# A four-layer convolution block on one core: the transfers of layer 2's mixing stage, put in the program's order and given other places in the loop

## The chip, the cores and the metric

The kernel runs on one core of one Trainium2 chip. The metric is the device time of one execution in microseconds (us). A core has five engines that follow their own instruction streams and meet through semaphores: PE (matrix multiply; its weight loads are listed apart as PEld), DVE and ACT (elementwise work), POOL (elementwise work) and SP, which here only issues transfers (DMAs) between the core's memory and the chip's large memory. "Granted clock" is the share of PE's full clock that the chip allowed. A name with a line, such as L970, is a line of the kernel before.

## The reference, cut to what matters

Sixteen images of 16 channels and 256x256 points go through four layers, each `x = x + layer(groupnorm(x))`. Layers 0, 1 and 3 are convolutions. Layer 2 is a Laplace operator in the frequency domain, and its part that matters here is this:

```python
alpha = jnp.fft.fft2(x, axes=(-2, -1))
A = 1.0 / (omega1[:, None, None, None] - weights_pole1[None])
Bm = 1.0 / (omega2[:, None, None, None] - weights_pole2[None])
S = jnp.einsum('ikpq,oikp,xikq->oxik', weights_residue, A, Bm)
output_residue1 = jnp.einsum('biox,oxik->bkox', alpha, S)
```

For every pair of frequencies (o, x), a 16x16 complex matrix S mixes the 16 input channels of `alpha` into 16 output channels, for all images. This is the "mixing". Because the input is real, only 129 of the 256 frequencies x are computed.

## The kernel before, in words

The kernel is one program of five stages, one after the other: layers 0 and 1; layer 2's forward transform, which writes `alpha` to a scratch tensor `alphad`; layer 2's mixing, which reads `alphad` and writes `mixd`; layer 2's transform back, which reads `mixd`; and layer 3. The change is in the third, the mixing (L860 to L1022).

**Rows.** The mixing runs over 64 steps, `for n in range(NF)` at L963, here called rows; one row is four frequencies o with all their 129 frequencies x. A row multiplies a tile `z` (128 partitions, `alpha` of the row) by a tile `sk` (the matrices S of the row). There are two `z` tiles, `zs[0]` and `zs[1]`; row n uses `zs[n % 2]`. Two matrices S are made at a time, for rows 2m and 2m+1, while the two rows before them are mixed.

**Groups.** A row has 32 positions (`for at in range(PX)`), four small products each (L970, written to `ps_m`), and so four groups g = 0 to 3 of eight positions. At the end of a group ACT copies half of `ps_m` to `other` (L996), and DVE adds and subtracts the two halves into the row's result tile `ob` (two instructions, L998, listed under the helper's line L190). `ps_m` has two buffers, `ob` has two.

**Making S beside it.** Each `next(steps, None)` runs one step of the generator `system` (L876): eight matmuls of one tile `ps_s` on PE (L891), then two steps that copy it into `sk`, on ACT (L899, L903, L908) for three tiles of four and on DVE for the fourth (`turns = "ADAA"`). One group takes three such steps, so one tile.

**Transfers of a row.** `reload(n, f)` (L927) brings in one quarter of the `z` tile of row n: DVE sets one column of that quarter (`V.memset`, L930), and SP issues the load of 258 KB (L917). `leave(n, part)` (L920) has SP issue the store of one quarter of `ob` of row n, 256 KB (L924). A row has four loads and four stores. In row n the program calls `reload(n + 1, 0)`, `leave(n - 1, 1)`, `reload(n + 1, 1)` and `leave(n - 1, 2)` at the end of group 0, `reload(n + 1, 2)`, `leave(n - 1, 3)` and `reload(n + 1, 3)` at the end of group 1, and `leave(n, 0)` at the end of group 3.

**What sets the order.** Instructions of an engine named in `tc.manual_schedule` stand in the order in which the program calls them; for the others a scheduler decides. Before, PE, DVE, ACT and POOL are named and SP is not. In the program as built, SP's stream in this stage is, for every row, four loads L917 and then four stores L924. Each engine works through its stream in order, and a transfer waits on SP for what it needs; a transfer also waits there for the one that stands eight transfers ahead of it, whose semaphore it uses again. A load of `z` needs PE to be done with the tile; a product needs all four loads of its row; a write to `ob` needs the four stores of the row two before.

**First and last rows.** Row 0's tile holds two rows of padding values which POOL clears at the end of row 0 (L992). Rows 62 and 63 have no S to make. After row 63 the stage leaves its last stores and the next stage's tables are loaded.

## Time and profile before

| | |
|---|---|
| time, median of 3 runs (lowest to highest) | 4326.98 us (4321.13 to 4331.19) |
| the profiled execution: its own time, its span | 4332.44 us, 4330.7 us |
| granted clock over the span | 0.955 |
| the mixing stage's rows 2 to 62 | 2302 to 3007 us of the span |
| transfers issued in these 705 us | 244 loads of `z`, 246 stores of `ob`, 186 GB/s |

The profile is of one execution. Its page gives each engine's busy time, and groups of instructions with the idle time of the engine just before them and what ended it. The view of the waits sums these idle times by who waited for whom. A wait "<-issue" is idle time for which the profile shows no cause. The timeline lists instructions in order of time, merged where they are alike; the number in brackets is the idle time before. Matmuls are pipelined on PE, so the durations of single matmuls overlap and a row "x64 in 1.10 us" is a run of 64.

### The profile page before, as it was taken

The page shows a single profiled execution, that of the slowest core. Times are in us where ns is not written, and L with a number is a line of the kernel's source. Part 1 is how long each engine was busy: PE and PEld are TensorE (multiplying, and loading weights), DVE is VectorE, ACT ScalarE, POOL GpSimd, SP SyncE. Part 2 cuts the span into 40 slices and gives each one's busy share as a digit, 9 for nine tenths or more (in the row PEclk, how much of TensorE's full clock was granted, in tenths as well). Part 3 has the DMA queues.
Part 4 walks back from the last instruction along what each step waited for, and adds up shares of the span by engine and source line. Part 5 has one row for each costly group of instructions (what it writes and reads, how often), then busy time and mean ns, then how long its engine had stood idle before and what let it go on. Part 6 is the DMA issues. An engine that isn't in the chain of part 4 may idle for free. (4 is left out here: it accounts for less than half of the span.)

```text
span 4330.7 us, 126404 instructions
## 1 busy us (share of the span) xinstructions
PE 3739.1 (86%) x52880; PEld 2882.1 (67%) x52880; DVE 3040.5 (70%) x5585; ACT 2573.2 (59%) x3641; POOL 2057.0 (47%) x3279
## 2 busy tenths in 40 slices
PE   4999999999967989999996777776899999996776
PEld 1455555555545989899985555555788888883444
DVE  4676667666659878787765566664567777768888
ACT  2868686776824434344446666665545544447898
POOL 2233232423244645564546666664566666662222
PEclk9999999999988999999999999998999999997989
DMA  6767676776633544444535666666878888877998
GB/s 141 172 154 191 142 192 150 183 169 155 158 89 117 164 144 144 139 152 157 162 113 167 182 194 183 185 192 174 228 217 239 237 244 235 247 206 273 343 351 295
DMA packets 479579, 820.78 MB, mean 190 GB/s; under 512 B 39648, under 2 KB 371424, under 8 KB 463584
## 3 DMA queue, kind: packets, MB, share of 16 engines
q1 hardware_dynamic: 431904, 644.63, 52.6%
q0 software_dynamic: 47104, 168.06, 13.0%
q8 instruction: 416, 6.82, 0.7%
q14 instruction: 155, 1.27, 0.1%
HBM read 408.85 MB, written 336.07 MB: 172 GB/s over the span
## 5 line engine op out<-in xcount | busy, mean ns | idle before, releaser
L382 PE MATMUL ps<-va,wt 128*64 128x512 f32 (+1 forms) x1632 | 668.7, 571 | 11.6 <-POOL va L354 9.2
L382 PE MATMUL ps<-vb,wt 128*64 128x512 f32 (+1 forms) x1632 | 667.1, 570 | 4.5 <-DMA vb<-va 4.5
L781 ACT ACTIVATE y<-ps_y,bc 128x384 f32<-128x384 f32 x512 | 296.4, 581 | 406.8 <-PE ps_y L779 406.6
L403 ACT ACTIVATE v<-xt,nm 32x2048 f32<-32x2048 f32 x248 | 497.2, 2005 | 9.8 <-PE ps L417 3.5
L417 PE MATMUL ps<-v,w1s 128*64 128x259 f32 x4096 | 486.4, 397 | 11.0 <-DVE v L401 6.7
L970 PE MATMUL ps_m<-z,sk 128*32 128x64 f32 x16384 | 334.5, 227 | 176.1 <-issue 126.5
L190 POOL TENSOR_TENSOR w<-rq 128x512 f32<-128x512 f32 x256 | 335.7, 1333 | 261.5 <-ACT rq L1115 259.4
L970 PEld LDWEIGHTS ps_m<-z,sk 128*32 128x32 f32 x16384 | 302.9, 114 | 227.2 <-issue 151.9
L382 PEld LDWEIGHTS ps<-va,wt 128*64 128x64 f32 x1632 | 223.1, 137 | 311.3 <-issue 283.3
L417 PEld LDWEIGHTS ps<-v,w1s 128*64 128x64 f32 x4096 | 338.9, 142 | 136.0 <-issue 27.9
L1114 PE MATMUL ps_o<-exp,fs 128*128 128x128 f32 x2048 | 399.6, 277 | 9.7 <-ACT fs L1162 9.7
L1113 PE MATMUL ps_o<-c_last,zt 128*128 128x128 f32 x2048 | 398.1, 276 | 0.0
L190 DVE TENSOR_TENSOR ob<-ps_m,other 128x256 f32<-128x256 f32 x512 | 192.9, 418 | 276.0 <-ACT other L996 262.4
L1259 PE MATMUL ps_c<-q,wt 64*64 64x512 bf16 (+1 forms) x4608 | 292.8, 405 | 108.6 <-ACT o L1306 91.7
L1113 PEld LDWEIGHTS ps_o<-c_last,zt 128*128 128x128 f32 x2048 | 323.2, 193 | 60.8 <-issue 60.8
L891 PE MATMUL ps_s<-t,l 128*32 128x258 f32 x4096 | 320.5, 401 | 42.3 <-issue 24.8
L190 POOL TENSOR_TENSOR acc<-acc,prod 128x256 f32<-128x256 f32 x240 | 232.8, 970 | 226.4 <-DVE prod L190 220.3
L1259 PEld LDWEIGHTS <-wt 64*64 64x64 bf16 x4800 | 181.6, 114 | 220.2 <-issue 152.8
L1114 PEld LDWEIGHTS ps_o<-exp,fs 128*128 128x128 f32 x2048 | 313.7, 194 | 11.3 <-ACT fs L1162 11.3
L776 PE MATMUL ps_y<-c_y,qd 128*128 128x128 f32 x2048 | 316.0, 277 | 1.6 <-ACT hat L738 1.6
L779 PE MATMUL ps_y<-hat,qd 128*128 128x128 f32 x2048 | 314.5, 276 | 0.0
L190 DVE TENSOR_TENSOR xt<-xt,ps 128x512 f32<-128x512 f32 x256 | 175.4, 685 | 187.6 <-PE ps L382 185.6
(234 smaller groups left out, 8897.9 us busy)
## 6 DMA issues: line engine op xcount, KB each, us to landing
xt<-x2d SPq DMA_DIRECT2D x256, 512.0 KB, 4.3
z<-alphad SPq DMA_DIRECT2D x258, 258.0 KB, 4.0
xt<-in_x_dram SPq DMA_DIRECT2D x256, 256.0 KB, 7.4
x2d<-x2s POOLq DMA_DIRECT2D x256, 256.0 KB, 5.0
mixd<-ob SPq DMA_DIRECT2D x256, 256.0 KB, 4.5
ot<-mixd SPq DMA_DIRECT2D x256, 256.0 KB, 6.2
x3d<-xt SPq DMA_DIRECT2D x128, 512.0 KB, 5.4
xt<-x3d SPq DMA_DIRECT2D x64, 1024.0 KB, 9.4
```

Source lines behind the costliest of these rows:

```text
L190: eng.tensor_tensor(o, a, b, op)
L382: nc.tensor.matmul(ps[halves[h], lo:hi, :], lhsT=wt0[:, w, :], rhs=v[:, 2 * t + lo : 2 * t + hi, j : j + N], start=j == 0 and k == 0, stop ...
L403: nc.scalar.activation(to, o.xt[c][q_], AF.Identity, bias=o.g.nm[q_, 1:2])
L417: nc.tensor.matmul(ps[halves[h], k, 0:U], lhsT=o.w1[:, w : w + 64], rhs=v1[:, lo : lo + U], start=first_, stop=not first_)
L776: nc.tensor.matmul(to[:, :, a, :], lhsT=v[:, c, a, i % 2, :], start=a == 0, stop=a == 1, rhs=y1[:, a].rearrange("p (r f) -> p r f", r=2))
L779: nc.tensor.matmul(ps[:, 2 * P : 3 * P], lhsT=v[:, c, a, i % 2, :], start=False, stop=a == 1, rhs=hats[0][:, a, i].rearrange("p r k -> p ( ...
L781: nc.scalar.activation(y[:, c, :], ps[:, 0 : 3 * P], AF.Copy, scale=bc2[:, b, i // 2, 0:1])
L891: nc.tensor.matmul(ps[at : at + 32, d, 0 : 2 * NX], lhsT=ls[h][:, k + d - k0, n], rhs=t2[:, h, k + d].rearrange("p r x -> p (r x)"), start ...
L970: nc.tensor.matmul(to, lhsT=sk[:, x_], rhs=z[:, :, x_], start=True, stop=True)
L1113: nc.tensor.matmul(ps[:, a, c, :], lhsT=zts[d][:, a, c, :], rhs=last[:, c, :], start=True, stop=False)
L1114: nc.tensor.matmul(ps[:, a, c, :], lhsT=fs[:, d, a, :], rhs=ey[:, d, c, :], start=False, stop=True)
L1259: nc.tensor.matmul(o, lhsT=wt[half[h], w, :], rhs=src, start=i == 0, stop=i == len(work[0]) - 1)
```

## The change

SP is put among the engines that keep the program's order in the mixing stage, and the calls are moved. The loads of row n+2, which go into the tile that row n has just used, now begin at the end of group 3 of row n. The order that SP gets, from the end of row n on, is load 0, store 0, load 1 at group 3 of row n; load 2, store 1, load 3 at group 0 of row n+1; and stores 2 and 3 of row n, which stand in the program at group 1 of row n+1 and need nothing that is not there before.

```diff
         es.enter_context(tc.manual_schedule(engines={
-            mybir.EngineType.PE, mybir.EngineType.DVE, mybir.EngineType.Activation, mybir.EngineType.Pool}))
+            mybir.EngineType.PE, mybir.EngineType.DVE, mybir.EngineType.Activation, mybir.EngineType.Pool,
+            mybir.EngineType.SP}))
...
-                    if n and g < 2:
-                        reload(n + 1, 2 * g)
-                        leave(n - 1, 2 * g + 1)
+                    if n and g == 0:
+                        reload(n + 1, 2)
+                        leave(n - 1, 1)
+                    if g == 3:
+                        reload(n + 2, 0)
+                        leave(n, 0)
...
                     next(steps, None)
-                    if n and g < 2:
-                        reload(n + 1, 2 * g + 1)
                     if n and g == 0:
+                        reload(n + 1, 3)
+                    if n and g == 1:
                         leave(n - 1, 2)
+                        leave(n - 1, 3)
                     if g == 3:
-                        leave(n, 0)
+                        reload(n + 2, 1)
```

In the programs as built, the streams of PE, ACT and POOL hold the same instructions in the same order before and after. DVE's differs in where the four one-column `memset` of a row stand, SP's in the order of its loads and stores. After the last row, SP's stream before has three of the next stage's small table loads ahead of row 63's four stores; after, these three stand behind them.

## The prediction

> **What bounds the kernel now.** I read the page first, then the busy time of the mixing rows, then who waits there, then the timeline of single rows.

> ```profile
> span 4330.7 us, 126404 instructions
> ...
> PE 3739.1 (86%) x52880; PEld 2882.1 (67%) x52880; DVE 3040.5 (70%) x5585; ACT 2573.2 (59%) x3641; POOL 2057.0 (47%) x3279
> ```

> The change touches one stage, so the page's averages decide nothing. The busy times of rows 2 to 62 alone (columns: stretch, its length, then busy us and count of PE, PEld, DVE, ACT and POOL, granted clock, DMA share, GB/s):

> ```profile
> 2302.00:3007.00 705.00, 505.41 (x19590) 409.43 (x19594) 419.07 (x1212) 478.34 (x1145) 423.48 (x1016) 0.96 0.64 186
> ```

> PE is busy 72% of the stage, ACT 68%, the transfers 64%. No engine is full. 64 rows end, by ACT's `other` copies, 11.5 us apart. What fills the rest is in the waits of the same stretch (us in total, times, longest), first PE's, then ACT's, then PEld's:

> ```profile
> PE ps_m L970 <- issue: 125.7, 88, 3.9
> PE ps_m L970 <- ACT sk L908: 31.2, 30, 1.7
> PE ps_s L891 <- issue: 24.8, 19, 2.1
> PE ps_m L970 <- DMA z<-alphad: 15.0, 16, 2.2
> ```

> ```profile
> ACT other L996 <- issue: 111.3, 65, 3.2
> ```

> ```profile
> PEld ps_m L970 <- ACT sk L908: 47.8, 34, 2.2
> ```

> The change can reach one of these directly, the 15.0 us in which PE waits for a load of `z`. The rest of PE's idle time is (a) "issue", 125.7 + 24.8 = 150.5 us, and (b) the wait of the even rows for ACT's last copy into `sk`. ACT in turn waits once in a row (65 times, 1.7 us each) for a product that PE has not issued, so a stop of PE does reach the other engines.

> What "issue" is, the packet records of the trace show. The queue of instructions carries these packets in the stage:

> ```profile
> q8 instruction: 155, 2.54, 1.5%
> ```

> That is 16 KB each. On the page there are 416 with 6.82 MB, and PE has 105,760 instructions: 64 bytes each, 256 in a packet. I read them as refills of PE's instructions. 154 of them start between 2302 and 3004; PE stops for 161 us in all, and starts again some 2.2 to 2.6 us after the packet's start: 1.05 us a refill. The stop goes with the traffic: 0.39 us where fewer than 5 data packets overlap the refill's first 0.9 us (27 refills), 0.82 with 5 to 30 (42), 1.08 with 30 to 60 (34), 1.49 with 60 to 90 (37), 1.73 with more (14). So moved transfers can also move this larger term.

> **The wait that goes.** SP's own timeline around rows 28 to 30:

> ```profile
> 2614.75 2.75 SPq L924 DMA_DIRECT2D mixd<-ob  x4
> 2617.61 4.22 SPq L917 DMA_DIRECT2D z<-alphad  x4
> 2626.26 1.64 SPq L924 DMA_DIRECT2D mixd<-ob  x2
> ```

> The four stores go as soon as a row ends; the four loads come behind, and each waits for its `memset`, the last until group 1 is done. Over rows 2 to 63 the last load is issued 3.0 to 6.9 us (mean 4.2) ahead of its row's first product, and a load of this kind lands 4.1 us after issue (2.8 to 5.8). In 27 of 62 rows the first product starts within 0.65 us of the last load's last packet; 25 of these are odd rows. Even rows wait for ACT's `sk` instead. Row 51 (odd), on PE:

> ```profile
> 2864.11 1.09 PE L970 MATMUL ps_m<-z,sk 128*32 128x64 f32 x60 [1.30 <-issue]
> 2865.04 1.66 PE L891 MATMUL ps_s<-t,l 128*32 128x258 f32 x16
> 2868.41 1.10 PE L970 MATMUL ps_m<-z,sk 128*32 128x64 f32 x64 [1.71 <-DMA z<-alphad]
> ```

> The eight matmuls for S are done, the products wait 1.71 us for the load. A refill began at 2865.25, so part of these 1.71 us would be a stop by refill anyway.

> **The change, part by part.**

> *Loads earlier.* After the change loads 0 and 1 go at the end of the row, and load 2 where load 0 is now: the issue of load 0 stands on average 4.3 us ahead of that of load 3. Load 3 then has load 2 and store 1 before it on SP, two issues of some 0.6 us, so it goes about 3.1 us earlier. The shortest distance becomes 3.0 + 3.1 = 6.1 us against a slowest landing of 5.8: the wait goes. Its worth is at most the 15.0 us. What passes on is open. From below: I set the time between `other` copies of eight groups against the refill stops inside them, and 0.32 us of each 1 us of stop shows up; over single groups and sums of two and four it is 0.36 to 0.54. From above: in the odd rows ACT has idle time in groups 0 and 1 beside nearly all of PE's wait (14.6 of 15.7 us), so all of it could pass. Ends: 15.0 x 0.32 = 4.8 and 15.0. I take 0.75, nearer the upper end, because the wait lies at the row's start, just ahead of ACT's idle time: **-11.2 us**. What is late next is `sk` from ACT for the even rows and the refills for all.

> *DVE.* The same four `memset`s of 0.06 us a row, in other places; each follows an `ob` add that already waited for PE, so none waits for more. One exception, once: at the end of row 0 the tile is cleared by POOL (L992, 2290.48 to 2294.02), and the `memset` of load 0 now stands on DVE ahead of row 1's first `ob` add, which ran at 2292.59. It moves to about 2294.2, its successor copy by about 0.75 us: PE's next product starts only at 2296.30. Between 0 and 1.6 us; I take **+0.7**.

> *SP.* Eight issues a row as before, some 5 us of 11.5. Load 0 waits for PE's last product, which the store behind it waits for too (through `ob`). Stores 1 to 3 now stand behind loads 2 and 3, so they leave 3 to 6 us later; `ob` of the row two later is first written some 14 us after the row's end, and a store lands in 4.5 us: nothing waits. At the end, row 63's stores stand ahead of three table loads instead of behind them; SP was busy from 3013.26 on without a gap and would now wait from about 3014.1 to 3014.85 for the last `ob` add, with the next stage's loads of `mixd` behind it: **+0.7**, between 0 and 1.

> *Traffic.* The same packets, in two bursts, 3 transfers at the row's end and 5 after group 0, and nothing in the last third of a row. Now: four stores at once, then the loads thinly. Stops by refill are now about 1.5 us in the stores' stretch (3 to 8 us after the row's end), 1.0 in the loads', 0.4 in the quiet one. After, I expect 1.3 in the first burst (2.7 us), 1.5 in the second (4.5 us), 0.4 in the quiet 4.3 us: (3.5 + 6.8 + 1.7) / 11.5 = 1.04, as now. **0**, with 154 x 0.12 = 18 us either way before it passes on.

> [...]

> Sum: -11.2 + 0.7 + 0.7 = **-9.8 us**. The profiled execution took 4332.4 us (span 4330.7), 5.5 above the median of 4327.0; I take the same off both: 4322.6 profiled, **4317** for the median.

> **The rivals.**

> *Both terms gain.* If the thinner first burst brings the mean stop to 0.9 us, 154 x 0.15 = 23 us, of which 0.45 pass on: -10 more, **4307**. For it: the stores at once are the worst stretch now. Against it: the second burst is five deep.

> *Wait replaced by wait.* If ACT's copies into `sk` decide every pair of rows (47.8 us of waits), an earlier odd row only waits longer at the next even one. At the lower end, -4.8 + 1.4 = -3: **4324**. For it: the share of 0.32.

> *Slower: denser traffic against the refills.* If in both bursts a refill stops PE as it now does among more than 90 packets (1.73 us for 7.2 us of the row, 0.39 for the rest), the mean is 1.23 us: 154 x 0.18 = 28 us, of which 0.45 to all passes on, 13 to 28. With -9.8: +3 to +18, say **4338**. The point: a mean stop over 1.19 us eats the gain at a share of 0.45, over 1.11 at a share of one.

> *It does not do what it says.* Load 3 could still land late, behind store 1 in the same DMA engines: then **4328**. The margin of 6.1 against 5.8 us speaks against it.

> **How the numbers follow.** Forecast 0.45, both gain 0.23, wait replaced 0.16, slower 0.13, not done 0.03. Changes under 0.2% (8.7 us) are about what a measurement of this kernel cannot tell from none. The forecast's own spread (-5 to -15) puts about 0.33 beyond -8.7 and 0.12 short of it: faster 0.33 + 0.23 = 0.56; same 0.12 + 0.16 + 0.03 = 0.31; slower 0.13. The range runs from 4300, both terms at -15 + 1.4 - 18 x 0.75 = -27, to 4332, which leaves out the upper part of the slower case and little below.

> **What would show it.** Right: PE's wait for `z` under 2 us; the last load issued over 6 us ahead of its product; "issue" of PE within 15 us of 150; `ACT sk` waits of PE up by no more than 5 us; the rows' mean 0.16 us shorter. Wrong: "issue" over 170 or under 130, `sk` waits that take the 15 us over, or any wait for a store.

## The result: slower by 0.25%

| | before | changed |
|---|---|---|
| median (lowest to highest) of 20 runs each, on one chip | 4326.67 us (4318.1 to 4342.15) | 4337.02 us (4320.85 to 4349.84) |
| ratio | | 1.0025 [1.0013, 1.0036] |
| the profiled execution, its span | 4332.44, 4330.7 us | 4334.06, 4332.3 us |
| mixing stage alone, first to last `other` copy of ACT | 739.3 us | 756.2 us |
| the same in a second profile of each (e10, e4 below) | 738.6 us | 752.4 us |

The forecast was 4317 us. The stage grew by 14 to 17 us. In the profiled execution the other stages, whose program is the same, took 15 us less, so its own time hides this; the medians do not (+10.4 us, where the 20 runs of one kernel spread over 24 to 29 us). From here on I compare the stage, which each kernel has from two profiles.

The page of the changed kernel shows nothing of it, as the one of before did not:

```profile
span 4332.3 us, 126406 instructions
...
PE 3739.2 (86%) x52880; PEld 2895.7 (67%) x52880; DVE 3041.0 (70%) x5585; ACT 2572.8 (59%) x3641; POOL 2061.1 (48%) x3279
```

The busy times of 2302 to 3007 us (length, then busy us and count of PE, PEld, DVE, ACT and POOL, clock, DMA share, GB/s):

```profile
2302.00:3007.00 705.00, 505.54 (x19179) 417.53 (x19171) 409.36 (x1189) 473.25 (x1133) 417.82 (x1002) 0.94 0.60 182
```

Read the counts: in the same 705 us PE ran 19179 matmuls, not 19590, so 2% less of the stage was done. What PE, PEld and ACT waited for there (us, times, longest):

```profile
PE ps_m L971 <- issue: 152.8, 99, 2.9
PE ps_m L971 <- ACT sk L908: 22.9, 23, 1.7
PE ps_s L891 <- issue: 21.1, 16, 2.5
```

```profile
PEld ps_m L971 <- ACT sk L908: 38.8, 30, 2.2
```

```profile
ACT other L997 <- issue: 130.7, 71, 3.2
```

The line `DMA z<-alphad` of 15.0 us is gone: the change does what it says. The waits for `sk` did not take its place; they fell from 31.2 to 22.9 us. But "issue", which the prediction read as stops at refills of PE's instructions, rose from 150.5 to 152.8 + 21.1 = 173.9 us (in the second profile of the changed kernel to 182.9). SP's timeline shows what is new beside them:

```profile
2601.48 0.47 SPq L917 DMA_DIRECT2D z<-alphad  x1
2602.05 0.54 SPq L924 DMA_DIRECT2D mixd<-ob  x1
2602.68 2.05 SPq L917 DMA_DIRECT2D z<-alphad  x2
2604.79 0.58 SPq L924 DMA_DIRECT2D mixd<-ob  x1
2605.46 0.55 SPq L917 DMA_DIRECT2D z<-alphad  x1
2606.07 2.41 SPq L924 DMA_DIRECT2D mixd<-ob  x2
```

Loads and stores now alternate, where before four stores left together and four loads thinly after them.

**Where PE stops.** The same stretch of the program on PE, first before, then changed (start, us, instructions, idle time before them):

```profile
2604.51 0.74 PE L970 MATMUL ps_m<-z,sk 128*32 128x64 f32 x33
2607.29 0.58 PE L970 MATMUL ps_m<-z,sk 128*32 128x64 f32 x26 [2.04 <-issue]
...
2618.68 0.44 PE L970 MATMUL ps_m<-z,sk 128*32 128x64 f32 x13
2620.77 0.92 PE L970 MATMUL ps_m<-z,sk 128*32 128x64 f32 x50 [1.66 <-issue]
...
2624.65 0.30 PE L970 MATMUL ps_m<-z,sk 128*32 128x64 f32 x3 [1.24 <-issue]
```

```profile
2603.72 0.75 PE L971 MATMUL ps_m<-z,sk 128*32 128x64 f32 x33
2605.00 0.58 PE L971 MATMUL ps_m<-z,sk 128*32 128x64 f32 x26 [0.54 <-issue]
...
2616.65 0.44 PE L971 MATMUL ps_m<-z,sk 128*32 128x64 f32 x13
2618.71 0.92 PE L971 MATMUL ps_m<-z,sk 128*32 128x64 f32 x50 [1.63 <-issue]
...
2623.69 0.30 PE L971 MATMUL ps_m<-z,sk 128*32 128x64 f32 x3 [2.34 <-issue]
```

PE breaks off at the same instruction in both: after the 33rd matmul of a run, after the 13th of another, three before the end of a third. Only the length of the stop differs. Counted over rows 2 to 61, every "issue" stop of PE over 0.3 us (104 before, 108 after) stands where PE's instruction count, its weight loads, matmuls and semaphore instructions together, leaves the same remainder of 256, or at the matmul of the weight load that stands there. So PE's work comes in **blocks of 256 instructions**, and a row (651 such records) is 2.54 of them. The instruction queue carries one packet of 16,384 bytes for each: 153 and 152 start in these rows, for 153 blocks, and in the whole span there are 416 in either kernel for 106,572 such records of PE, 256.2 a packet. I read each packet as the refill that brings the next block, and call *delay* the time from a block's first instruction to that packet's start. Where PE then stops (107 of 153 blocks before, 112 after), it goes on 2.44 us after that packet's start, in both kernels. The mean block took 4.54 us before and 4.65 after (4.62 in the second profile); times 2.54 these are the rows of 11.56 and 11.84 us in another unit. The mean delay went from 1.95 and 1.98 us before to 2.09 and 2.07 after: 0.09 to 0.14 us x 153 blocks = 14 to 21 us, the size of the loss. Each of these means has a standard error of some 0.05 us, so the delays alone would be thin evidence. But within each trace the delay and the block go together: over the blocks of one profile, 1 us more delay makes the block 0.66 to 0.88 us longer.

### The profile page after: what moved, and what is told of

Same layout as the page of the kernel before. It is cut to its first block, busy times and chain, and to the rows that moved or that the text cites. A ratio compares the mean times of both kernels' runs of the same rounds, so it can differ in the third digit from the quotient of the medians.

```text
span 4332.3 us, 126406 instructions
## 1 busy us (share of the span) xinstructions
PE 3739.2 (86%) x52880; PEld 2895.7 (67%) x52880; DVE 3041.0 (70%) x5585; ACT 2572.8 (59%) x3641; POOL 2061.1 (48%) x3279
## 3 DMA queue, kind: packets, MB, share of 16 engines
q8 instruction: 416, 6.82, 0.7%
q14 instruction: 155, 1.27, 0.1%
## 5 line engine op out<-in xcount | busy, mean ns | idle before, releaser
L971 PE MATMUL ps_m<-z,sk 128*32 128x64 f32 x16384 | 348.1, 231 | 184.0 <-issue 154.7
L971 PEld LDWEIGHTS ps_m<-z,sk 128*32 128x32 f32 x16384 | 316.7, 117 | 231.8 <-issue 177.2
L891 PE MATMUL ps_s<-t,l 128*32 128x258 f32 x4096 | 325.9, 409 | 39.0 <-issue 21.1
```

Source lines behind the costliest of these rows:

```text
L891: nc.tensor.matmul(ps[at : at + 32, d, 0 : 2 * NX], lhsT=ls[h][:, k + d - k0, n], rhs=t2[:, h, k + d].rearrange("p r x -> p (r x)"), start ...
L971: nc.tensor.matmul(to, lhsT=sk[:, x_], rhs=z[:, :, x_], start=True, stop=True)
```

## The experiments

All are compared with the kernel before on the same chip. Rows 2 to 61, from one profile each (the waits for `z` from 2302 to 3007 us, in e10 to 2980); "both" counts the blocks, of 153, in which loads and stores were under way together 1 us after the block's start (issued on SP and not fully landed):

| kernel | ratio of times | row us | PE's wait for z, us | delay us | block us | both |
|---|---|---|---|---|---|---|
| before / again (e10) | 1 | 11.56 / 11.56 | 15.0 / 11.9 | 1.95 / 1.98 | 4.54 / 4.54 | 29 / 27 |
| changed / again (e4) | 1.0025 [1.0013, 1.0036] | 11.84 / 11.78 | 0 / 0 | 2.09 / 2.07 | 4.65 / 4.62 | 114 / 118 |
| e1 order only | 1.0161 [1.0142, 1.0181] | 12.78 | 66.2 | 2.19 | 5.04 | 110 |
| e2 loads, then stores | 0.9948 [0.9931, 0.9965] | 11.24 | 0 | 1.92 | 4.41 | 50 |
| the same again (e11) | 0.9949 [0.9932, 0.9966] | 11.29 | 0 | 1.89 | 4.44 | 47 |
| e3 stores, then loads | 1.0003 [0.9994, 1.0012] | 11.60 | 5.3 | 2.03 | 4.56 | 31 |
| e7 e2 with one store early | 1.0004 [0.9990, 1.0017] | 11.77 | 0 | 2.04 | 4.62 | 97 |
| e8 all at the row's end | 0.9982 [0.9970, 0.9993] | 11.53 | 0 | 1.92 | 4.53 | 56 |
| e5 before, no loads | 0.9888 [0.9870, 0.9906] | 10.77 | - | 1.67 | 4.25 | 0 |
| e6 changed, no loads | 0.9891 [0.9871, 0.9911] | 10.72 | - | 1.67 | 4.23 | 0 |
| e9 stores held | 1.0128 [1.0109, 1.0146] | 12.42 | 0 | 1.98 | 4.88 | 25 |
| e12 fewer PE instructions | 1.1294 [1.1269, 1.1318] | 20.12 | 0 | - | 9.9 | - |
| e13 more PE instructions | 1.0216 [1.0187, 1.0244] | 13.13 | 0 | 1.77 | 4.31 | - |

The theory I started with: loads and stores under way together hold up the refills, and half clock after long stops (51 us of rows 2 to 61 before, 82 in the changed kernel) adds to it. The rivals: the depth of the bursts, the early loads themselves, or the moved `memset`s.

**e1, the order alone.** The kernel before with SP among the ordered engines and every call where it was.

```diff
-            mybir.EngineType.PE, mybir.EngineType.DVE, mybir.EngineType.Activation, mybir.EngineType.Pool}))
+            mybir.EngineType.PE, mybir.EngineType.DVE, mybir.EngineType.Activation, mybir.EngineType.Pool,
+            mybir.EngineType.SP}))
```

> Only the order is changed: SP follows the program, the calls stay where they were before, so loads and stores alternate one to one and the loads begin as late as before. Theory (mixing): where loads and stores share the queues, PE's refills take longer (mean stop 1.20 us against 1.12 in the traces of after and before), more of the 3.41 us stretches fall under about 0.42 of PE busy and are followed by one at half clock; then this is slower by about 10 us, with over 70 us of half clock in rows 2 to 61 and PE busy over 8.45 us a row. Rival (early loads): what costs is that the loads begin earlier; then this stays within 5 us of before, with 50 us of half clock.

It lost 71 us (4393.28 against 4322.58), far more than expected. PE's waits in 2302 to 3007:

```profile
PE ps_m L971 <- issue: 82.8, 64, 3.7
PE ps_m L971 <- DMA z<-alphad: 66.2, 29, 3.9
```

The loads come late behind stores, and PE stands for `z` at times when it would have stood for a refill. The block grew by 0.50 us: 0.24 of that is delay, the rest stands behind the refill's start, where the wait for `z` falls. So the order alone does harm in both ways, and the early loads of the change mend one of them. The time at half clock is also longer here (167 us against 51 in rows 2 to 61), and its part is not separated.

**e2, the change's loads with all stores behind them.**

```diff
                     if n and g == 0:
                         reload(n + 1, 2)
-                        leave(n - 1, 1)
                     if g == 3:
                         reload(n + 2, 0)
-                        leave(n, 0)
...
                         reload(n + 1, 3)
-                    if n and g == 1:
-                        leave(n - 1, 2)
-                        leave(n - 1, 3)
+                        for part in range(4):
+                            leave(n - 1, part)
...
```

> The loads begin as early as in the changed kernel (0 and 1 at the end of the row, 2 and 3 after group 0), the four stores follow in one block behind load 3. Nothing is mixed, but the loads are early and six transfers are issued in a row. Theory (mixing): no slower than before, mean stop at a refill at most 1.12 us, half clock about 50 us, 4315 to 4327 us. Rival (early loads): slower by about 10 us as the changed kernel is. Second rival (deep burst): slower than the changed kernel, since six instead of five transfers stand behind one another.

**Faster than both kernels**, by 0.52% of before, and again by 0.51% in a second measurement with its own profile (e11: 4298.74 against 4322.87 us):

> The version with loads first and the four stores behind them once more, with a second trace. Theory: 4297 to 4309 us, 11.2 to 11.35 us a row, a mean delay of 1.88 to 1.96 us, both pending at 40 to 60 of 153 boundaries. If the median lies above 4315 us the first measurement was chance.

SP's timeline of e2, and PE's waits in 2302 to 3007 us (its stage ends before that, so the sums are of the whole rest of it):

```profile
2608.59 3.84 SPq L917 DMA_DIRECT2D z<-alphad  x4
2612.53 3.68 SPq L924 DMA_DIRECT2D mixd<-ob  x4
2617.93 4.83 SPq L917 DMA_DIRECT2D z<-alphad  x4
2622.84 3.52 SPq L924 DMA_DIRECT2D mixd<-ob  x4
```

```profile
PE ps_m L971 <- issue: 126.7, 101, 2.9
PE ps_m L971 <- ACT sk L908: 24.4, 26, 1.6
PE ps_s L891 <- issue: 19.5, 17, 2.0
```

The same early loads and `memset`s, deeper bursts, and no store between two loads: the stage takes 718.2 us. So neither the early loads nor the depth of the bursts is what costs; it is the places of the stores. How these act is another question, taken up below.

**e3, the four stores at once at the row's end, then the change's loads.**

```diff
...
                     if g == 3:
+                        for part in range(4):
+                            leave(n, part)
                         reload(n + 2, 0)
-                        leave(n, 0)
...
```

> The stores stay in one block at the end of the row, as before; loads 0 and 1 stand right behind them and loads 2 and 3 wait for group 0 instead of group 1. Theory (mixing): refills as before (mean stop 1.12 us, half clock about 50 us), PE's wait for the loads falls from 15 us to under 4, so 5 to 10 us faster than before. Rival (early loads): slower by about 10 us. Second rival (deep burst): slower, six transfers in a row.

A miss: no gain (1.0003). PE's waits:

```profile
PE ps_m L971 <- issue: 145.9, 93, 3.4
PE ps_s L891 <- issue: 21.1, 18, 2.2
...
PE ps_m L971 <- DMA z<-alphad: 5.3, 4, 1.9
```

Ten us of the wait for `z` go (15.0 to 5.3), and "issue" rises from 150.5 to 167.0. So taking that wait away is not enough for a gain.

**e4 and e10, second profiles of the changed kernel and of before.**

> The changed kernel once more, for a second trace: how far refills and half clock vary from one execution to the next. Theory: again 70 to 95 us of half clock in rows 2 to 61, mean stop 1.15 to 1.25 us, 11.75 to 11.95 us a row. If half clock comes out near 50 us with the rows as long, the clock is not the cause.

> The kernel before once more, for a second trace: refills, waits and half clock from one execution to the next. Theory: PE's wait for the loads 12 to 18 us, mean delay of a refill 1.90 to 2.00 us, 11.5 to 11.6 us a row; half clock may vary by 25 us without the rows becoming longer by more than 0.1 us.

PE's waits in e4, 2302 to 3007:

```profile
PE ps_m L971 <- issue: 155.7, 99, 3.2
PE ps_s L891 <- issue: 27.2, 19, 2.7
```

Rows, delays, blocks and "both" repeat (table). What does not repeat is the time at half clock: 82 us in the first profile of the changed kernel, 58 in the second, 51 and 41 before, with rows of 11.84 and 11.78 against 11.56. The second pair differs by 17 us of half clock in place of 31, and its rows by 0.22 us in place of 0.28. So that part of my theory is not the main cause; a smaller share of it is not excluded.

**e5 and e6, both kernels without loads.**

```diff
-                load(n, f, f)
+                if n < 2:
+                    load(n, f, f)
```

> The kernel before without the loads of z for rows 2 to 63 (the memsets stay): these rows mix the values of rows 0 and 1 again, so the output is not the reference's; the time is what counts. Theory (refill): PE runs out of instructions at every 256th; a block of 256 takes the delay until its refill starts (1.4 us with no transfer pending, 1.9 with loads or stores alone, 2.3 with both) plus some 2.45 us. Without loads the mean delay falls from 1.95 to about 1.65, a row from 11.56 to about 10.4 us, the kernel to 4250 to 4270 us. Rival (ACT and DVE set the pace beside the waits): less than 20 us gained, the 15 us wait and little more.

> The changed kernel without the loads of z for rows 2 to 63 (the memsets stay), so with stale values in them. Theory (refill): what the change costs needs loads and stores pending together; without loads it comes within 6 us of the kernel before without loads. Rival (places of the memsets, or the clock): it stays 10 us or more slower than that one.

4274.49 and 4281.39 us: the ratios, 0.9888 and 0.9891, are the same within their intervals. In e6 no load stands ahead of the stores on SP. With equal traffic (102 GB/s in e5 and 103 in e6, from 2302 to 2900 us) no price of the `memset`s' places is seen: the stage takes 691.4 us in e5 and 687.0 in e6. The intervals, some 8 us either way, would not show a small one; e2, which has the `memset`s where the changed kernel has them and is faster, says the same. And all the loads from row 2 on together are worth 48 us of the stage (739.3 to 691.4).

**e7, e2 with one of its stores ahead.**

```diff
...
                     if g == 3:
                         reload(n + 2, 1)
+                        leave(n, 0)
...
```

> As the version with loads first and the four stores behind them (4303 us), but store 0 stands behind load 1 at the end of the row, ahead of loads 2 and 3. Theory (refill): the boundaries of PE's blocks at which loads and stores are both pending rise from 50 of 153 toward the changed kernel's 116; 4310 to 4330 us. Rival: only a store between two loads of one burst costs; then within 5 us of 4303.

One store of four between the second and the third load takes the gain away: 4326.06 us against 4303.03, row 11.77 against 11.24. "Both" goes from 50 to 97. The profiled execution, 4331.65 us, was one of the longer ones: by its row e7 would be as slow as the changed kernel, by its median it equals before.

**e8, loads and then stores, all eight at the row's end.**

> All four loads, then all four stores, at the end of the row: one burst of eight, and a long quiet stretch after it. Theory (refill): both pending at no more boundaries than with loads first in two bursts (50 of 153), more boundaries with nothing pending (over 40), mean delay 1.8 to 1.9 us: 4285 to 4305 us. Rival (deep burst): eight transfers behind one another delay a refill more, over 2.0 us in the mean, and it is slower than 4315 us.

Faster by 0.18%, less than e2. The delays are uneven: 2.65 us where both kinds are under way, which is also where most is under way, 1.45 where nothing is and 1.58 with one kind. A short delay is worth less than it seems: PE stops in only about half of the blocks with a delay under 1.6 us, and such a block lasts 2.8 us past its delay, where one with over 2.5 us lasts 2.4.

**e9, stores held back** by a small transfer that waits for a later `memset`, two stores in each of groups 1 and 2.

> As the version with loads first and the four stores behind them (4303 us), but the stores are held: 0 and 1 until group 1 ends, 2 and 3 until group 2 ends, each pair by one column set by DVE and a transfer of 64 bytes that waits for it. So the same bytes lie thinner over the row, and loads and stores are pending together less often. Theory (refill, set by what is pending together): both pending at fewer than 40 of 153 boundaries, mean delay 1.75 to 1.9 us, a row of 11.0 to 11.3 us, 4290 to 4305 us. Rival (a quiet last third is what helps, since a refill there starts after 1.4 us): with no quiet stretch left the mean delay is over 1.95 us and it is slower than 4315 us.

It kept loads and stores apart (25) and was of no use otherwise. DVE's and PE's largest waits, in 2302 to 2980:

```profile
DVE ob L190 <- DMA mixd<-ob: 192.3, 45, 7.1
...
PE ps_m L978 <- DVE z L930: 69.8, 46, 3.3
```

The stores leave so late that DVE stands for `ob`, and PE behind it. So its time says nothing on the theory. Its delay does: "both" fell to 25, but the mean delay was 1.98 us, not the 1.75 to 1.9 expected.

**e12 and e13, other numbers of PE instructions, on e2's order.** e12 merges the third and fourth product of a position into one with a weight tile of 64 columns; e13 issues the fourth product twice.

```diff
-                for a in range(4):
+                for a in (0, 1, 2, 3, 3):
```

> As the version with loads first and the four stores behind them (4299 and 4303 us, 11.24 and 11.29 us a row), but the products of the last two of the four positions are one matmul with two neighbouring matrices on the values of the first of them: a quarter of the row's results are wrong, and PE has 128 instructions fewer a row, 520 instead of 648, so 2.03 instead of 2.53 blocks of 256. All transfers and the work of ACT, DVE and POOL are the same. Theory (refill): a row takes 2.03 blocks of 4.4 to 4.6 us, 8.95 to 9.35 us, unless another engine stops it first; the stage is 120 to 145 us shorter, the kernel 4155 to 4185 us. Rival (PE's own work sets the pace, and the stops only fill waits for other engines): a quarter of the 4.4 us of products goes, 1.1 us a row: 10.1 us a row, the kernel 4225 to 4235 us.

> As the version with loads first and the four stores behind them (4299 and 4303 us, 11.24 and 11.29 us a row, refill delay 1.9 us), but each position's fourth product is issued twice in a row, into the same place: 128 PE instructions more in a row, 776 instead of 648, so 3.03 instead of 2.53 blocks of 256. Transfers and the work of ACT, DVE and POOL are the same, and PE's new work is 32 products of the kind of which 128 take 4.4 us. Theory (a refill for every 256 instructions sets the pace): half a block more, 0.5 x 4.3 to 4.45 us = +2.15 to +2.2 us a row, 13.4 to 13.5 us a row, the kernel 4430 to 4445 us. Rival (PE's own work sets the pace, the stops only fill waits for other engines): +1.1 us a row, 12.3 to 12.4 us, the kernel 4365 to 4375 us.

e12 cannot tell, for another reason. Its products no longer overlap (windows 2302 to 2900, then PE's timeline):

```profile
2302.00:2900.00 598.00, 588.30 (x7715) 384.82 (x7714) 205.01 (x595) 234.00 (x568) 210.31 (x506) 0.99 0.34 106
```

```profile
2600.24 0.31 PE L971 MATMUL ps_m<-z,sk 128*32 128x64 f32 x4
2600.47 0.33 PE L991 MATMUL ps_m<-z,sk 128*64 128x64 f32 x2
```

These six matmuls take 0.56 us, from 2600.24 to 2600.80, where a run of 64 took 1.10. So the row became 20.12 us long, not 9 or 10. PE is 98% busy, a block lasts 9.9 us, and its stops at block ends vanish (0.02 us on average), so in blocks of this length the refills cost next to nothing.

In e13 the repeated product does not overlap either, so PE's work grew by 2.97 us a row (8.28 to 11.25), not by the little I had reckoned with. Still the row grew by only 1.87, since PE's idle time fell:

```profile
PE ps_m L971 <- issue: 69.6, 83, 1.9
...
PE ps_s L891 <- issue: 11.5, 21, 1.8
```

A row is now 651 + 128 = 779 instructions, 3.04 blocks of 4.31 us. Of such a block 1.77 us is delay and 2.54 the rest, as in the other kernels (2.55), though PE's own work in a block grew from 3.26 to 3.70 us. That fits a pace set by refills; but since PE's work and the delay changed together, it does not prove it by itself. The row of 13.13 us lies between the two expectations.

## Why the prediction was wrong, point by point

1. **"The wait goes."** Right: 15.0 us to 0. The margin was smaller than I reckoned: the last load was issued 4.4 to 9.6 us ahead of its product (mean 7.2), not at least 6.1.
2. **"I take 0.75 ... -11.2 us."** Not settled. Taking the delay off the block leaves 2.59 and 2.56 us before, 2.56 and 2.55 changed, 2.53 in e3, 2.49 and 2.55 in e2 and e11: the wait's end is worth 0 to 0.10 us a block, so 0 to 15 us, and the -11.2 lies in that range. The wait stood partly inside stops by refill, as row 51 had shown; the share should have come from those refills and not from ACT's idle time.
3. **Traffic: "0".** This is the step that failed. The mean stop at a refill was to stay at 1.04 us. It grew by 0.06 to 0.15 us (point 4). The sum of 3.5 + 6.8 + 1.7 counts on two bursts that are over after 2.7 and 4.5 us, and on 4.3 quiet us in a row. By the packet records of the changed kernel's two profiles, nothing was under way in only 1.5 us of a row, and less than 100 KB in 2.6 us (before: 1.0 and 1.6 us): load 3 and the last store are issued some 5 and 7 us after the row's end, and a store takes 4.4 us to land. With 2.6 quiet us my own stop lengths give (3.5 + 1.5 x 6.5 + 0.4 x 2.6) / 11.8 = 1.21 in place of 1.04, more than enough for the loss. So in the prediction's own terms the quiet stretch was mis-sized: 4.3 us where 2.6 came. This is no full account of the order, though: e2 has still less quiet time (0.7 and 1.5 us by the same two counts) and shorter stops.

   There may be a second part, the mixture. Loads and stores were under way together in 29 blocks of 153 before, and in 114 and 118 in the changed kernel. The delay by what is under way 1 us after a block's start, two profiles each, us:

| | before, e10 | e2, e11 | changed, e4 |
|---|---|---|---|
| nothing | 1.52, 1.48 | 1.37, 1.36 | 1.42, 1.44 |
| 200 to 400 KB | 1.82, 1.73 | 1.64, 1.74 | 2.15, 2.02 |
| 400 to 700 KB | 1.91, 1.97 | 1.84, 1.77 | 2.15, 2.31 |
| over 700 KB | 2.25, 2.33 | 2.34, 2.27 | 2.40, 2.29 |

   The amount counts, and I had that. At 200 to 700 KB the changed kernel's delays are 0.2 to 0.5 us longer for the same amount. That a mixture as such costs this is not shown. In e5 and e6, where only stores move, the delays are 2.09 and 2.02 us at 400 to 700 KB and 2.41 and 2.49 above. In e7 the 30 mixed blocks of 400 to 700 KB have 1.99. A straight line through the blocks of all profiles but e12's gives 1.38 us, and 0.27 and 0.30 us for each 256 KB of loads and of stores; whether both are under way adds 0.06, with a standard error of 0.03. Against e2 the changed kernel's delay is 0.15 to 0.20 us longer at the same mean amount (535 to 547 KB), so the order does count beyond the amount.
4. **The rival "denser traffic against the refills"** is what came, at 4338 for 4337, though density alone is not its reason: e2's bursts are deeper, and faster. Its point was a mean stop of 1.11 us at a share of one. On a window a little wider than the prediction's (the stop that ends 2.0 to 3.5 us after the refill's start), which gives 1.12 and 1.15 for the two profiles of before, the stop is 1.21 and 1.27. That is 0.06 to 0.15 us more for 154 refills, 9 to 23 us, and the stage lost 14 to 17 although the wait for `z` was gone: most of it passes on, rather than 0.45.
5. **"Both terms gain"** was near, but needs another order: e2, 0.52% below before. On the same window the stop is 1.03 and 1.04 us in e2 and e11.
6. **"Wait replaced by wait"** at `sk`: did not come. The terms of DVE and SP (0.7 us each): too small to be seen; e5 against e6 shows no price for the `memset`s within some 8 us.
7. The sign to look for, "issue" over 170, was the right one: 173.9.

**Open:** why a refill starts later in the alternating order, by the longer bursts, the mixture or both; and why e2's delay is short for its amount. The records show when each packet starts and how long it takes, not why one starts ahead of another. How much of e2's gain is delay is open too: 0.09 of 0.10 us a block in e11 against e10, but 0.03 of 0.13 in e2 against before.

## What to carry to other kernels

Where an engine's idle time is "issue" without a releaser, look whether it stops at the same instruction each time; if so, time per block of instructions is the unit (here 256 of PE's, 4.54 us before), and part of a transfer's price is what it adds to the wait for the refill (here a mean delay of 1.67 us without loads in e5, 1.95 with them). When moved transfers are to leave a quiet stretch, reckon it from issue and landing times, not from the bursts' intended lengths (here 4.3 us reckoned, 2.6 measured). Put loads together and stores together, loads first where they are due first: here that order is worth some 0.8% against the alternating one (0.9948 to 1.0025), with the same transfers. Before a removed wait is counted as a gain, see whether the engine would have stood there anyway (here 15.0 us of waits went, for 0 to 15 us).
